# Attention and tree feed-forward on one core: which PSUM bank a tile gets is chosen by a count of each engine's work

## The chip, the cores and the metric

The kernel runs on one core of a Trainium2 chip. The metric is the device time of one execution in microseconds (us), smaller is better. TensorE is called PE, its weight loads PEld, VectorE DVE, ScalarE ACT, GpSimd POOL and SyncE, which issues the DMAs, SP.

## The reference

Eight sequences of 512 tokens and 256 features pass through four residual layers, each behind a layer norm:

```python
x = x + attn_a(layernorm(x), ...)   # 16 heads of 16, biases, every key is seen
x = x + ffn(layernorm(x), ...)
x = x + attn_b(layernorm(x), ...)   # 16 heads of 16, rotary embedding, causal
x = x + ffn(layernorm(x), ...)      # the same weights as above
```

`attn_a` and `attn_b` are softmax(q k / sqrt(16)) v with an output projection. `ffn` is a soft decision tree of depth 8: gate = sigmoid((x Wq) routers), 255 gates a token; the probability of each of 256 leaves is the product of the gates (or one minus the gate) on its path; the result is leaf_prob @ leaf_values, projected by Wout with a bias. All is in float32.

## The kernel before, in words

The work is cut into 16 blocks n: n = 0 to 7 are the sequences' first attention and tree, n = 8 to 15 the causal attention and the tree again. The main loop at the end of `hybrid_kernel` goes over steps i. Every step issues, in this order:

- `scores`: four PSUM tiles named st, one for each of four row groups of 32 partitions (four heads side by side), k times q in two passes and a third that subtracts the row maximum from rows in m. ACT then takes exp of each tile into pt (L599); in the causal blocks POOL masks pt (L604).
- `maxima`: four PSUM tiles named mx, q times k in two passes, one tile for each row group. DVE takes the largest of each row (L554 non-causal; L549 in the causal blocks, with the mask). This runs some seven steps ahead of the scores.
- `weigh`, once in four or fewer steps: the tile av, pt times v, copied by ACT (L621).
- other units of work, put between by tables of due steps written out by hand (BEFORE, BEHIND, OUTPUT, CHAINS): the projections v, q and k, the output projection y, the gates z, the tree's product ty and the transposes xt, txt and lt, each with a PSUM tile of its own.

`passes` issues the four tiles' first matmuls, then their second, and so on, so that the four row groups work at the same time:

```python
    for i in range(last + 1):
        for parts in todo:
            ps, lhsT, rhs = parts[part][i]
            nc.tensor.matmul(ps, lhsT=lhsT, rhs=rhs, start=i == 0, stop=i == last)
```

Its matmuls are L516 in the profile, of mx and st alike. Those of v, y, z and ty are L376 (`by_tokens`), of the transposes L350, of q and k L418 and L490, of av L616.

Who reads a PSUM tile: ACT reads st (L599), av (L621), the transposes (L351, L359), v (L458), z (L727, tanh) and the non-causal q and k (L426). DVE reads mx (L554, L549), adds y and ty to x (L669) and multiplies the causal q and k with cosine and sine (L498). DVE also multiplies the tree's paths (L756, lp<-th,lp), which reads no PSUM.

Every PSUM tile comes from `bank`. There is one pool of eight buffers under one tag, and each tile fills a whole bank:

```python
    banks = ctx.enter_context(tc.tile_pool(name="banks", bufs=8, space=PSUM))
    def bank(shape, name):
        return banks.tile(shape, F32, tag="ps", name=name)
```

The framework's pool chooses which of the eight buffers a tile gets when it builds the program, and puts semaphore waits on the tile's first matmul for the last reader of the buffer's former tile. After the whole program is written, `in_program_order` ties each engine's instructions to the order in which they were written, so no instruction overtakes another on its engine.

## Time and profile before

| | |
|---|---|
| median of 3 runs | 1142.22 us (1135.12 to 1142.41) |
| the profiled execution | 1138.38 us |
| its span | 1136.5 us |
| PE busy | 1047.8 us, 92% |
| DVE busy | 835.5 us, 74% |
| ACT busy | 630.2 us, 55% |
| POOL busy | 435.4 us, 38% |
| mean granted PE clock | 0.971 |

The span is the time from the first to the last instruction that the profiler recorded; the execution's own time has 1.9 us around it. All rows come from one profiled execution. In lists of groups, a row gives the line, engine, operation, output and input tiles with their shapes, the number of instructions, then busy time, mean ns of one instruction, and the idle time of the engine just before them with what ended most of it. In the timeline, a row gives the start, the duration of a run of like instructions, and in brackets the idle time before it and its releaser. PE matmuls overlap one another in the records, and their ends are modelled.

### The profile page before, as it was taken

Reading aid. Unit: us, or ns where it says so; the run is one execution under the profiler, and the core shown is the slowest. Engines: PE = TensorE matmul, PEld = TensorE weight load, DVE = VectorE, ACT = ScalarE, POOL = GpSimd, SP = SyncE. Lnnn points to the kernel's source line nnn. Section 1 sums busy time; section 2 is a strip of 40 time slices with the busy share of each in tenths; the row PEclk is TensorE's granted clock in tenths of the full one; section 3 lists DMA queues with packets and bytes.
Section 4 is the critical chain, followed back from the end, with each engine's and each line's share of the span. In section 5 each row is a group of like instructions: output and inputs, shape, how many; then the busy total and the mean of one; then the engine's idle time right before and its main releaser. Section 6 shows DMA issues by size and latency. Waiting matters only on the chain. (4 is left out here: it accounts for less than half of the span.)

```text
span 1136.5 us, 24276 instructions
## 1 busy us (share of the span) xinstructions
PE 1047.8 (92%) x8916; PEld 608.4 (54%) x8916; DVE 835.5 (74%) x2368; ACT 630.2 (55%) x1329; POOL 435.4 (38%) x600
## 2 busy tenths in 40 slices
PE   5999999999999999999999898999999999999886
PEld 2544454554545545455454555656555565556555
DVE  4867586767767777777867868887878787887735
ACT  2466666666666666666474544554455455545441
POOL 2221332222412224122325464655456465554242
PEclk9999999999999999999999999999999999999799
DMA  8110302104031040321222304131221404140111
GB/s 305 66 59 18 132 22 103 42 17 164 22 117 60 21 164 23 128 74 36 96 78 75 102 29 148 41 125 67 100 87 43 140 22 152 40 146 23 41 36 56
DMA packets 69671, 91.48 MB, mean 80 GB/s; under 512 B 15025, under 2 KB 36273, under 8 KB 69553
## 3 DMA queue, kind: packets, MB, share of 16 engines
q1 hardware_dynamic: 69552, 89.94, 22.9%
q8 instruction: 70, 1.15, 0.4%
q14 instruction: 49, 0.39, 0.1%
HBM read 20.71 MB, written 8.91 MB: 26 GB/s over the span
## 5 line engine op out<-in xcount | busy, mean ns | idle before, releaser
L599 ACT ACTIVATE pt<-st 128x512 f32<-128x512 f32 (+1 forms) x896 | 435.0, 573 | 205.3 <-PE st L516 203.7
L554 DVE TENSOR_REDUCE most<-mx 128x1 f32<-128x512 f32 x512 | 317.0, 682 | 120.1 <-PE mx L516 119.8
L549 DVE CUSTOM_DVE_ANT_0 seen<-mx,mask 128x128 f32<-128x128 f32 (+3 forms) x512 | 250.5, 489 | 85.6 <-PE mx L516 37.9
L516 PE MATMUL mx<-k,q 32*128 32x512 f32 (+3 forms) x2048 | 221.2, 395 | 35.4 <-DVE most L549 10.6
L616 PE MATMUL av<-pt,v 128*32 128x512 f32 (+3 forms) x2048 | 200.2, 531 | 6.4 <-DVE x L669 2.8
L516 PE MATMUL st<-q,k 32*128 32x512 f32 (+3 forms) x2048 | 187.4, 402 | 2.8 <-DVE most L549 1.8
L516 PEld LDWEIGHTS mx<-k,q 32*128 32x128 f32 x2048 | 128.4, 187 | 90.3 <-DVE most L549 23.0
L604 POOL TENSOR_SCALAR_AFFINE_SELECT pt<-pt 128x256 f32<-128x256 f32 (+1 forms) x192 | 97.7, 517 | 165.3 <-ACT pt L599 163.1
L388 POOL TENSOR_TENSOR hl<-r,hl 128x512 fp32r<-128x512 f32 x62 | 80.2, 1300 | 179.8 <-ACT hl L426 168.8
L516 PEld LDWEIGHTS st<-q,k 32*128 32x128 f32 x2048 | 90.7, 185 | 108.5 <-issue 69.4
L616 PEld LDWEIGHTS av<-pt,v 128*32 128x32 f32 x2048 | 62.7, 112 | 131.0 <-issue 94.5
L621 ACT COPY o<-av 128x512 f32<-128x512 f32 x64 | 37.5, 586 | 137.3 <-issue 106.5
L516 PE MATMUL st<-m,ones 32*128 32x512 f32 (+3 forms) x1024 | 101.2, 356 | 0.0
L756 DVE SCALAR_TENSOR_TENSOR lp<-th,lp 128x8 f32<-128x8 f32 (+7 forms) x238 | 74.5, 350 | 3.8
L502 POOL TENSOR_TENSOR r<-r,r 128x512 f32<-128x512 f32 x32 | 41.4, 1303 | 85.9 <-DVE r L498 85.9
L376 PE MATMUL ty<-wl,lpT 128*128 128x256 f32 x256 | 67.6, 416 | 2.4 <-ACT lpT L359 1.4
L376 PE MATMUL z<-wg,txnT 128*128 128x255 f32 x256 | 63.1, 390 | 3.4 <-ACT pt L599 2.5
L418 PE MATMUL qk<-xnT,a_qk 128*128 128x512 f32 x128 | 63.4, 624 | 0.9 <-ACT pt L599 0.7
L662 POOL TENSOR_TENSOR out<-out,den 128x512 f32<-128x512 f32 x31 | 40.4, 1304 | 61.2 <-DMA den<-apart 55.1
L490 PE MATMUL qk<-xnT,b_qk 128*128 128x512 f32 x128 | 59.4, 605 | 2.9 <-ACT xnT L351 2.5
L516 PEld LDWEIGHTS st<-m,ones 32*128 32x128 f32 x1024 | 57.5, 185 | 6.5 <-DMA m<-rows 0.7
L376 PEld LDWEIGHTS ty<-wl,lpT 128*128 128x128 f32 x256 | 51.4, 207 | 15.0 <-issue 2.8
(86 smaller groups left out, 1075.2 us busy)
## 6 DMA issues: line engine op xcount, KB each, us to landing
q<-hl SPq DMA_DIRECT2D x128, 256.0 KB
k<-hl SPq DMA_DIRECT2D x64, 256.0 KB
out<-o SPq DMA_DIRECT2D x64, 128.0 KB
den<-apart SPq DMA_DIRECT2D x32, 256.0 KB
x<-x SPq DMA_DIRECT2D x8, 512.0 KB
between<-x SPq DMA_DIRECT2D x8, 512.0 KB
x<-between SPq DMA_DIRECT2D x8, 512.0 KB
out<-x SPq DMA_DIRECT2D x7, 512.0 KB
```

The source lines that it names most:

```text
L376: nc.tensor.matmul(ps[:, i, :n], lhsT=srcT[:, c, (t + i) * P : (t + i + 1) * P], rhs=w[:, c, :], start=c == 0, stop=c == NC - 1,)
L388: on.tensor_tensor(hl[:, 1, :], raw, hl[:, 0, :].bitcast(F32), ALU.subtract)
L418: nc.tensor.matmul(ps, lhsT=(w.q, w.k)[which][:, k, c * P : (c + 1) * P], rhs=xnT[:, k, :], start=k == 0, stop=k == NC - 1,)
L490: nc.tensor.matmul(ps, lhsT=wt[:, k, c * P : (c + 1) * P], rhs=xnT[:, k, :], start=k == 0, stop=k == NC - 1,)
L502: nc.gpsimd.tensor_tensor(raws[c], raws[c], raws[2 + c], (ALU.subtract, ALU.add)[c])
L516: nc.tensor.matmul(ps, lhsT=lhsT, rhs=rhs, start=i == 0, stop=i == last)
L549: nc.vector.tensor_tensor_reduce(out=seen[:, :width], in0=ps, in1=mask[:, S - width :], scale=1.0, scalar=LOWEST, op0=ALU.add, op1=ALU.max ...
L554: nc.vector.tensor_reduce(at, ps, AX.X, ALU.max)
L599: nc.scalar.activation(pt[:, i, :at], ps[:, :at], AF.Exp, scale=SCALE)
L604: nc.gpsimd.affine_select(out=blocks, in_=blocks, pattern=[[0, 2], [0, len(kts)], [1, P]], compare_op=ALU.is_ge, fill=0.0, base=0, channel ...
L616: nc.tensor.matmul(av[32 * j : 32 * j + 32, first:], lhsT=vs[n % 2][:, kt, g * NJ + j, :, :].rearrange("p d s -> p (d s)"), rhs=pts[j // 2 ...
L756: nc.vector.scalar_tensor_tensor(pairs[:, :, :, side], of_level, one, lp[:, part, :], ALU.add, ALU.mult)
```

## The change

Instead of one pool with eight buffers there is one pool with a single buffer under each of eight tags, ps0 to ps7, and a class `Banks` that names the tag. While the program is written it keeps a running count of time for PE, ACT and DVE. `take` gives a tile the bank whose expected free time is the smallest, and moves PE's count to that time if it is behind. `work` adds a cost to an engine's count. `read` says who reads a tile and for how long: the reader's count becomes the later of itself and PE's count plus LATE, plus the cost, and the bank is expected free LATE after that. The costs are six constants in us. Everything happens when the program is built; the calls of `work` and `read` are spread over the functions that issue matmuls and readers. POOL has no count, and a few operations of ACT and DVE that read no PSUM are not counted.

```diff
+PASS, PRODUCT, COPY, REDUCE, CHANGE, LATE = 0.25, 0.89, 0.58, 0.69, 0.15, 0.1
+class Banks:
+    def __init__(self, pool):
+        self.pool = pool
+        self.free = [0.0] * 8
+        self.taken = {}
+        self.at = dict(pe=0.0, act=0.0, dve=0.0)
+
+    def take(self, shape, name):
+        k = min(range(8), key=lambda i: self.free[i])
+        self.at["pe"] = max(self.at["pe"], self.free[k])
+        self.free[k] = float("inf")
+        t = self.pool.tile(shape, F32, tag=f"ps{k}", name=name)
+        self.taken[id(t)] = (k, t)
+        return t
+
+    def work(self, engine, cost):
+        self.at[engine] += cost
+
+    def read(self, t, *costs):
+        k, _ = self.taken.pop(id(t))
+        for engine, cost in costs:
+            self.at[engine] = max(self.at[engine], self.at["pe"] + LATE) + cost
+        self.free[k] = max(self.at[e] for e, _ in costs) + LATE
...
-    banks = ctx.enter_context(tc.tile_pool(name="banks", bufs=8, space=PSUM))
+    banks = Banks(ctx.enter_context(tc.tile_pool(name="banks", bufs=1, space=PSUM)))
-    def bank(shape, name):
-        return banks.tile(shape, F32, tag="ps", name=name)
+    bank = banks.take
...
     # layer_norm, for each of four tiles
+            banks.work("dve", COPY)
...
     # transposed
+        banks.work("pe", PRODUCT)
+        banks.read(ps, ("act", COPY))
...
     # by_tokens, then v, z and the adds of y and ty to x
+            banks.work("pe", count * PRODUCT)
+                banks.read(ps, ("act", count * COPY / 2))
+            banks.read(ps, ("dve", count * REDUCE / 2))
...
     # causal q and k
+                banks.work("pe", 2 * PRODUCT)
+                banks.read(ps, ("dve", 2 * REDUCE))
...
     # passes, once for each pass over the four row groups
+                banks.work("pe", PASS * todo[0][part][i][2].free_size() / S)
...
     # maxima
+        banks.work("pe", CHANGE)
+        for whole, parts in zip(blocks, got):
+            banks.read(whole, ("dve", sum(REDUCE * (width + 80) / (S + 80) for _, width, _ in parts)))
...
     # scores
+                banks.read(ps, ("act", COPY * (at + 80) / (S + 80)))
...
     # weigh
+        banks.work("pe", CHANGE + sum(PRODUCT * (S - first) / S for _, _, first in group))
+        banks.read(av, ("act", COPY))
...
     # the tree's levels
+                banks.work("dve", 0.1 + len(ts) * m * 0.002)
```

More of the change, by code (lines that the diff above doesn't have):

```diff
@@ L276, in chains @@
                     )
+                banks.work("pe", PRODUCT)
+                banks.read(ps, ("dve" if to is wl else "act", COPY))
                 if to is wl:
@@ L291, in fold_bias @@
         nc.vector.tensor_tensor(out_b, ps, out_b, ALU.add)
+        banks.work("pe", PRODUCT)
+        banks.read(ps, ("dve", COPY))
         folded.append(True)
@@ L351, in transposed @@
         nc.scalar.copy(dst[:, c, :], ps.rearrange("p t q -> p (t q)"))
+        banks.work("pe", PRODUCT)
+        banks.read(ps, ("act", COPY))
     def transposed_half(dst, src, ts, name):
@@ L359, in transposed_half @@
         nc.scalar.copy(dst[:, :, ts[0] * P : ts[0] * P + 2 * P], ps.rearrange("p c t q -> p c (t q)"))
+        banks.work("pe", PRODUCT)
+        banks.read(ps, ("act", COPY))
     def by_tokens(srcT, w, n, name, evict, times, ts=range(NT)):
@@ L426, in block @@
             nc.scalar.activation(to, ps, AF.Identity, bias=w.qk_b[:, at : at + 1])
+        banks.work("pe", 2 * PRODUCT)
+        banks.read(ps, ("act", 2 * COPY))
         return raw, hl
@@ L498, in pre @@
                     nc.vector.tensor_tensor(raws[-1], ps, table, ALU.mult)
+                banks.work("pe", 2 * PRODUCT)
+                banks.read(ps, ("dve", 2 * REDUCE))
             if causal:
@@ L528, in maxima @@
         most = lesses[n, g]
-        got, todo = [], []
+        got, todo, blocks = [], [], []
+        banks.work("pe", CHANGE)
         for j in range(NJ):
@@ L532, in maxima @@
             rows = slice(32 * j, 32 * j + 32)
+            blocks.append(ps)
             got.append([])
@@ L569, in put @@
         nc.scalar.copy(rows, ps)
+        banks.work("pe", PASS)
+        banks.read(ps, ("act", COPY / 2))
         nc.sync.dma_start(ms[g % 2].bitcast(F32)[:: HD, :], rows)
@@ L647, in divide @@
         inv = pool2.tile([P, S // HD], F32, tag="inv", name=f"inv{n}_{c}")
+        banks.work("dve", COPY)
         nc.vector.reciprocal(inv, few[:, c, :])
@@ L729, in gates @@
             )
+            banks.read(ps, ("act", count * COPY / 2))
         yield from by_tokens(xnT, wg, NODES, f"z{n}", gates, when(n, "z"), ts)
```

## The prediction

> **What bounds the kernel now.** I read the page's busy shares first, then busy time by stretch, then the costliest groups, and then followed the PSUM banks tile by tile through the timeline: of each tile, when the last reader of the bank's former tile ended and when the tile's own first matmul began.

> ```profile
> span 1136.5 us, 24276 instructions
> PE 1047.8 (92%) x8916; PEld 608.4 (54%) x8916; DVE 835.5 (74%) x2368; ACT 630.2 (55%) x1329; POOL 435.4 (38%) x600
> ...
> L599 ACT ACTIVATE pt<-st 128x512 f32<-128x512 f32 (+1 forms) x896 | 435.0, 573 | 205.3 <-PE st L516 203.7
> L554 DVE TENSOR_REDUCE most<-mx 128x1 f32<-128x512 f32 x512 | 317.0, 682 | 120.1 <-PE mx L516 119.8
> ...
> L516 PE MATMUL mx<-k,q 32*128 32x512 f32 (+3 forms) x2048 | 221.2, 395 | 35.4 <-DVE most L549 10.6
> ```

> PE is busy 92% and idle 88.7 us. ACT and DVE mostly wait for PE, and PE in its turn waits ahead of mx matmuls: short waits for a reader to give a bank back. The idle column understates them, since a matmul whose four row groups do not start together still counts as busy. By the bank bookkeeping 576 of 2229 tiles start within 0.15 us of their bank's release, 0.05 to 0.06 us behind it, and the matmuls of these groups start some 130 us later in all than in groups whose banks were free.

> ```profile
> 40.00:570.00 530.00, 504.67 (x4092) 269.04 (x4096) 387.88 (x800) 341.66 (x688) 146.93 (x169) 1.00 0.21 73
> 570.00:1075.00 505.00, 466.70 (x4395) 291.56 (x4386) 395.65 (x1424) 259.72 (x585) 258.61 (x375) 0.96 0.24 82
> ```

> (Columns: stretch, its length, busy time of PE, PEld, DVE, ACT, POOL, granted clock, DMA share, GB/s.) The first row is the non-causal stage, the second the causal one. DVE's share is 73% and 78%: near enough to full that DVE's queue, not the choice of a bank, ends many PE waits.

> **The change part by part.** *Eight pools and the count.* They add no instruction: compiled, each engine has the same instructions in the same order as before, no DMA issue is moved past another, and all 2229 tiles come in the same order. Only the bank of a tile differs, and with it the reader that its first matmul waits for: 1054 tiles follow another tile than before in their bank. Price of the code itself: 0.

> *What a choice can be worth.* Four mx or st tiles form a group, whose second pass is issued behind the first pass of all four, so the latest of four banks sets the group. At the times of this trace the best possible choice would take 16.1 us off these waits. The new choice takes 11.4 us off 14 larger and 6 small groups, and makes 47 groups later by 20.9 us together. What remains is to say which of both survive.

> *Loss 1, the projection y.* In the stretch where y is interleaved with the last two mx groups of a sequence, the timeline shows:

> ```profile
> 487.77 0.93 PE L516 MATMUL mx<-k,q 32*128 32x512 f32 x8
> 488.51 2.48 DVE L554 TENSOR_REDUCE most<-mx 128x1 f32<-128x512 f32 x4 [0.60 <-PE mx L516]
> 488.63 1.99 PE L376 MATMUL y<-a_o,out 128*128 128x256 f32 x8
> 490.55 0.74 PE L516 MATMUL st<-q,k 32*128 32x512 f32 x8
> 490.91 0.68 DVE L669 TENSOR_TENSOR x<-y,x 128x512 f32<-128x512 f32 x1
> 491.35 1.02 PE L516 MATMUL mx<-k,q 32*128 32x512 f32 x8
> 491.55 2.06 ACT L599 ACTIVATE pt<-st 128x512 f32<-128x512 f32 x4 [1.52 <-PE st L516]
> 491.65 0.29 PEld L516 LDWEIGHTS mx<-k,q 32*128 32x128 f32 x5 [0.33 <-DVE x L669]
> 492.30 1.99 PE L376 MATMUL y<-a_o,out 128*128 128x256 f32 x8
> ```

> The fourth mx tile takes y's bank: the add ends at 490.91 + 0.68 = 491.59, the tile starts at 491.64. The changed kernel gives it the bank of the first st tile, whose exp ends at 491.55 + 0.60 = 492.15: it starts 0.55 late (492.20). In the next group (495.32) the same swap costs 0.61. Why the count errs, from the start of the earlier mx group: it puts y's release at 4.35 us (four reads of REDUCE 0.69, where the trace has 2.48/4 = 0.62; two LATE) and the exp's at 4.01 (its PE takes 2.47 to the st group); the trace has 3.82 (487.77 to 491.59) and 4.38. It is off by 0.53 one way and 0.37 the other, and turns a lead of 0.56 into a lag of 0.34. Behind the late tile stand pass two, then y (1.99, held by PE alone), then st, whose exps and reads start at fixed distances behind PE; nothing there has the slack to give the time back, and DVE and ACT, which wait 0.6 and 1.5 us here, are only later too. Sequences 1 to 6: 6 x (0.55 + 0.61) = 7.0; sequence 7: 0.25 + 0.61 = 0.9. Sum 7.9 us.

> *Loss 2, other non-causal groups.* Two with ty in y's place (0.69, 0.68) and two small ones (0.25, 0.18) stand ahead of PE work as well: 1.8, taken as 1.6. Those early in sequences 0 and 1 (0.36, 0.32, 0.57, 0.81) come ahead of a group that waits longer for its reader anyway: 0, and 2.1 if that cover is missing.

> *Loss 3, causal.* The third mx group's bank moves to v's copy or the last sequence's first exps (2.3 over six sequences, kept 1.9); single groups at 709.38 (0.51), 1031.49 (kept 0.55 of 0.90), 1072.88 (kept 0.4 of 0.69), 637.19 (kept 0.3 of 0.51): together 3.7, taken as 3.6. The rest (st groups of 0.2, lessT, 626.30, 632.30; 3.1) is ahead of a longer wait for DVE: 0 under that cover.

> *Gains.* The largest repeats in five causal sequences:

> ```profile
> 744.43 0.32 PE L516 MATMUL mx<-k,q 32*128 32x128 f32 x1 [0.32 <-DVE r L498]
> 745.63 0.72 PE L516 MATMUL mx<-k,q 32*128 32x128 f32 x13 [0.87 <-DVE r L498]
> 745.49 1.39 DVE L756 SCALAR_TENSOR_TENSOR lp<-th,lp 128x512 f32<-128x512 f32 x1
> 750.20 1.28 DVE L669 TENSOR_TENSOR x<-ty,x 128x512 f32<-128x512 f32 x2
> ```

> The fourth tile would start 0.97 earlier, 5 x 0.97 = 4.9 us. But DVE works without a gap from 743.10 to 751.48; its reads of these tiles stand behind lp and cannot come earlier. PE gains 0.97 and stands at the next mx group, whose third tile waits for the second ty add (ends 751.48, tile starts 751.53) whenever PE arrives. So 0, with 4.9 as the other bound. Kept are one group at 665.53, where DVE itself is idle 0.89 for PE (1.0), and about half of the 2.03 at 1054.40, where the next bank's reader then binds (1.0): 2.0. Six non-causal gains of 0.3 to 0.5 come, like the covered losses, ahead of a longer wait: 0, at most 2.3.

> *Sum.* 7.9 + 1.6 + 3.6 - 2.0 = +11.1 us. The profiled execution took 1138.38 us with a span of 1136.5 (1.9 around it, unchanged): 1149.5. Against the median of the runs shown, 1142.22, it would be 1153.3; of the four executions two lie at 1142.3, one at 1135.1 and this one at 1138.4. I say 1150.0, nearer the one whose steps I followed.

> [...] The row at 491.65 shows PE waiting for one bank's reader with seven others taken, and by it the choice counts.

> **The rivals.** *B, nothing is absorbed:* each late group costs PE what the trace says, since what follows it shifts as well: 1138.4 + 20.9 - 2.0 = 1157.3. For it: PE is at 92%. Against: DVE's 78% in the causal stage.

> *C, not slower:* the mis-picks of y are void, because in the changed run exp does end before y's add, as the count has it. From an order of 0.56 us the other way this decides: the add must come 0.56 later, or the exp earlier, than in the trace; the gains then stand whole, 1138.4 - 11.4 = 1127.0. For it: ACT has 45% idle. Against: exp and add hang on PE's starts with distances that repeat in seven sequences.

> *D, it does not do what it says:* DVE and ACT queues set the pace so far that any choice gives the same time; bank numbers are mostly labels: 1138.4 to 1142.2, within 2 us. For it: most changed tiles had a bank free long before in both kernels (only 72 tiles' new bank is still held at the trace's start of the tile). Against: the waits of 491.65 follow the reader at once.

> **How the numbers follow.** My forecast (+5 to +16 us, 1143 to 1158) 0.65, B 0.15, C 0.08, D 0.12. Predicted: 1150.0. The range goes from 1139 (losses half absorbed, or D) to 1160 (B with the runs' own spread). One per cent is 11.4 us, about what a measurement of this kernel can tell from no change. Faster: C, 0.08. Slower by over 1%: B and half of the forecast, 0.15 + 0.32 = 0.47. Within: 0.45.

> **What would show it.** In the changed profile, around the y motif, PEld or PE of mx should wait for ACT pt L599's new line instead of DVE x, about 0.85 us instead of 0.33, in sequences 1 to 7; PE waits for "DVE r" in the causal stage should fall by some 5 us while those for DVE's maxima and x adds grow by as much; DVE's and ACT's busy time should be unchanged, PE's idle time plus its stretched mx matmuls some 11 us higher, of them 9 before 570 us. I am wrong if y's add is not ahead of the exp there, if the non-causal stage is not longer, or if the causal stage is shorter by more than 2 us.

## The result, and the profile after

The changed kernel takes 1144.8 us (median of 20 runs) against 1138.57 us before (20 runs): ratio 1.0049, 95% interval 1.0028 to 1.0069, or +5.6 us (3.2 to 7.9). A second comparison (after_again, below) gave 1.0054. I had forecast +11.1 us: the sign held, and the size was twice what came.

The page of the changed kernel, profiled in an execution of 1147.6 us (its lines answer to those shown of before; line numbers moved):

```profile
span 1145.7 us, 24268 instructions
PE 1049.0 (92%) x8916; PEld 607.6 (53%) x8916; DVE 834.6 (73%) x2368; ACT 631.3 (55%) x1329; POOL 434.3 (38%) x600
...
L654 ACT ACTIVATE pt<-st 128x512 f32<-128x512 f32 (+1 forms) x896 | 435.0, 573 | 203.9 <-PE st L563 202.2
L606 DVE TENSOR_REDUCE most<-mx 128x1 f32<-128x512 f32 x512 | 317.3, 682 | 132.6 <-PE mx L563 131.9
...
L563 PE MATMUL mx<-k,q 32*128 32x512 f32 (+3 forms) x2048 | 230.7, 400 | 43.5 <-ACT pt L654 16.7
```

The work of every engine is what it was. The mx matmuls are 9.5 us longer in the records (221.2 to 230.7) and PE stands 8 us more ahead of them (35.4 to 43.5), the largest part now for ACT's exp. The list of PE's waits shows the exchange (engine, line, released by: us in total, times, longest):

```profile
PE mx L563 <- ACT pt L654: 16.7, 38, 1.2
PE mx L563 <- DVE most L601: 10.9, 28, 1.1
...
PE lessT L619 <- DVE less L611: 4.0, 6, 1.0
```

Of mx for ACT it was 2.7 us before, for DVE r (causal q and k) 10.4 and now 1.4, of av for DVE x 2.8 and now none among its longer waits. The wait of lessT for DVE is new.

The y motif of sequence 6, in the timeline of the changed kernel:

```profile
502.14 0.74 PE L563 MATMUL st<-q,k 32*128 32x512 f32 x8
...
502.50 0.68 DVE L727 TENSOR_TENSOR x<-y,x 128x512 f32<-128x512 f32 x1
...
502.94 0.41 PE L563 MATMUL mx<-k,q 32*128 32x512 f32 x3
503.13 2.06 ACT L654 ACTIVATE pt<-st 128x512 f32<-128x512 f32 x4 [1.63 <-PE st L563]
503.78 0.29 PEld L563 LDWEIGHTS mx<-k,q 32*128 32x128 f32 x5 [0.87 <-ACT pt L654]
...
504.43 1.99 PE L417 MATMUL y<-a_o,out 128*128 128x256 f32 x8
```

y's bank is free at 502.50 + 0.68 = 503.18, but the fourth mx tile has the first st tile's bank, free at 503.13 + 0.60 = 503.73, and starts at 503.78: 0.55 late, as reckoned. The y behind it starts 0.55 late too.

Both kernels issue the same matmuls in the same order, so the start of each tile can be subtracted between the two traces. The changed kernel's delay is 1.4 us at 100 us, grows by 0.55 and 0.61 at the y groups of each of sequences 2 to 6, is 14.5 us where the causal stage begins (585 us), and then shrinks to 9.2 us. Two jumps of 1.7 us in it lie where the changed trace has half clock (granted clock 0.72 on the mean from 137 to 143 us of its own time, 0.66 from 347 to 352). The causal stage, where I expected +1.6, came out 5.3 us shorter in this pair of traces. That was one of the signs by which I had said I would be wrong. Not all of it is banks: the trace before spends 51.2 us of that stage at half clock, the changed one 37.5.

Ratios of the further runs, each against before on the same chip, in us of 1138.5:

| run | ratio | 95% interval | us |
|---|---|---|---|
| old_choice | 0.9994 | 0.9974 to 1.0014 | -0.7 |
| only_y | 1.0053 | 1.0028 to 1.0078 | +6.0 |
| not_y | 0.9975 | 0.9947 to 1.0002 | -2.8 |
| by_trace | 0.9969 | 0.9949 to 0.9989 | -3.5 |
| causal_new | 0.9988 | 0.9969 to 1.0008 | -1.4 |
| gains | 0.9983 | 0.9963 to 1.0004 | -1.9 |
| losses | 1.0042 | 1.0026 to 1.0059 | +4.8 |
| calibrated | 0.9973 | 0.9949 to 0.9997 | -3.1 |
| y_late | 1.0299 | 1.0266 to 1.0331 | +34.0 |
| rest_nc | 1.0021 | 1.0000 to 1.0041 | +2.4 |
| after_again | 1.0054 | 1.0025 to 1.0083 | +6.1 |
| warm_old | 0.9940 | 0.9916 to 0.9963 | -6.8 |
| warm_new | 1.0005 | 0.9984 to 1.0025 | +0.6 |
| warm_trace | 0.9909 | 0.9879 to 0.9938 | -10.4 |

### The profile page after: what moved, and what is told of

Its sections match the earlier page's. It is cut to its first block, busy times and chain, and to the rows that moved or that the text cites. A ratio compares the mean times of both kernels' runs of the same rounds, so it can differ in the third digit from the quotient of the medians.

```text
span 1145.7 us, 24268 instructions
## 1 busy us (share of the span) xinstructions
PE 1049.0 (92%) x8916; PEld 607.6 (53%) x8916; DVE 834.6 (73%) x2368; ACT 631.3 (55%) x1329; POOL 434.3 (38%) x600
## 5 line engine op out<-in xcount | busy, mean ns | idle before, releaser
L654 ACT ACTIVATE pt<-st 128x512 f32<-128x512 f32 (+1 forms) x896 | 435.0, 573 | 203.9 <-PE st L563 202.2
L563 PE MATMUL mx<-k,q 32*128 32x512 f32 (+3 forms) x2048 | 230.7, 400 | 43.5 <-ACT pt L654 16.7
L563 PE MATMUL st<-q,k 32*128 32x512 f32 (+3 forms) x2048 | 183.1, 403 | 2.4 <-DVE most L601 1.5
L676 ACT COPY o<-av 128x512 f32<-128x512 f32 x64 | 37.5, 586 | 144.8 <-issue 107.6
L549 POOL TENSOR_TENSOR r<-r,r 128x512 f32<-128x512 f32 x32 | 41.3, 1303 | 87.0 <-DVE r L543 87.0
L417 PE MATMUL ty<-wl,lpT 128*128 128x256 f32 x256 | 64.3, 400 | 3.6 <-ACT lpT L398 1.4
L360 POOL TENSOR_SCALAR ln_lesst<-ln_mvt 128x4 f32<-128x4 f32 (+1 forms) x17 | 4.1, 239 | 148.8 <-DVE ln_mvt L353 148.8
```

The lines of the kernel that those rows point to most:

```text
L417: nc.tensor.matmul(ps[:, i, :n], lhsT=srcT[:, c, (t + i) * P : (t + i + 1) * P], rhs=w[:, c, :], start=c == 0, stop=c == NC - 1,)
L549: nc.gpsimd.tensor_tensor(raws[c], raws[c], raws[2 + c], (ALU.subtract, ALU.add)[c])
L654: nc.scalar.activation(pt[:, i, :at], ps[:, :at], AF.Exp, scale=SCALE)
```

## The experiments

Most of them replace the count by a list: one digit, the bank, for each of the 2229 tiles. The list is the choice of one kernel, with exchanges of two banks' digits from some tile on.

```diff
+TABLE = ("0123456...", ...)
     def take(self, shape, name):
-        k = min(range(8), key=lambda i: self.free[i])
+        k = int(TABLE[len(self.seen)])
+        self.seen.append(name)
```

### The parts of the change

**old_choice**: the list of the kernel before.

> The class with its eight pools, but the banks are read from a list: the choice of the kernel before, tile by tile. Both theories (a late bank costs PE its time in full; part of it is given back by fewer stretches at half the PE clock): no change, ratio 1.000 within 0.003, and the profile's waits as before. If the eight pools cost something by themselves: about 1.005, as the changed kernel.

-0.7 us (-3.0 to +1.6), no change: no cost of eight pools of one buffer can be told from nothing, and 0.5% is excluded. What the change does is in who gets which bank.

**only_y**: that list, with 14 exchanges.

```diff
-    mx6_3_2_3 follows y5_0 in its bank       (and 13 like it)
+    mx6_3_2_3 follows st6_1_3_0
```

> The old choice from the list, with 14 exchanges alone: the fourth mx tile of the last two mx groups of sequences 1 to 7 gets the first st tile's bank, as in the changed kernel, instead of y's. By the trace these cost 7.9 us. Theory 1 (every late bank costs in full, the y groups are the bulk of the loss): ratio 1.007 (+7.9 us), and in the profile +1.16 us for each sequence. Theory 2 (the delays are there, but the clock gives part back: fewer or cheaper stretches of half clock): +1.16 us for each sequence outside those stretches, but the ratio only 1.003 to 1.005. Rival (the loss is elsewhere, in the causal stage): 1.000 to 1.002.

+6.0 us (3.2 to 8.9). In its trace the delay grows again by 0.55 and 0.61 at the y groups of each of sequences 2 to 6.

**not_y**: the changed kernel's list with the same 14 put back.

> The changed kernel's choice from a list, with the 14 fourth mx tiles behind y put back to the bank of the kernel before. Theory 1: 7.9 us less than the changed kernel; against before 1.0049 - 0.0069 = 0.998. Theory 2: about half of that is seen, 1.001. Rival (the loss is elsewhere): 1.004 or more.

-2.8 us, 8.4 below the changed kernel's +5.6. With only_y it brackets the 7.9 of the forecast: loss 1 stood. And it leaves a surprise: without the y tiles the change is not 3.2 us slower, as the rest of my sum says, but level or a little faster (-6.0 to +0.2).

**rest_nc** and **causal_new** split this rest: not_y's list up to 585 us and the old one behind it; the old list up to 585 us and the changed kernel's behind it.

> The changed kernel's choice of the non-causal stage without the 14 tiles behind y, and the old choice from 585 us on: what I called loss 2 and the early gains. By the trace of before 4.7 us later and 3.3 earlier. My sum kept 1.6 us of it: ratio 1.0014. If, as not_y (0.9975) less causal_new (0.9988) hints, nothing is lost there: 0.998 to 1.000.

> Old choice up to 585 us (from the list), the changed kernel's choice behind it: the causal stage alone, its losses and gains together. My sum for this stage (losses kept 3.6, gains kept 2.0): +1.6 us, ratio 1.0014. If the stage gives back more than I counted, which not_y at 0.9975 hints at: -2 to -4 us, 0.997 to 0.998. If nothing of the gains stands and all losses do: +7 us, 1.006.

The non-causal rest costs 2.4 us (1.6 forecast), the causal stage -1.4 (+1.6 forecast). only_y, rest_nc and causal_new add up to +7.0; the whole was +5.6 and +6.1. So the choice of banks divides into parts that add up, within their intervals, and the one part that lies outside the forecast by more than its interval (-3.5 to +0.9) is the causal stage.

**losses** and **gains** divide that stage once more.

> Old choice, with only the changed kernel's later banks in the causal stage (third mx group, first mx groups at 709.4 and 1031.5 us, st groups, lessT; 7.8 us by the trace of before). My count: those ahead of a longer wait for DVE are absorbed, 3.6 us stay, 1.003. If nothing is absorbed: 1.007. If DVE's queue absorbs all: 1.000.

> Old choice, with only those ten exchanges of the changed kernel that make a causal bank come free earlier: five mx groups behind the causal q and k (4.9 us), three av tiles (3.0), the mx group at 665.5 us (1.1) and the st group at 1054.4 us (2.0). No tile waits longer than before by the trace of before. If a wait ahead of a busy DVE is only moved, as I reckoned for the first five and would for av: -2 to -3 us, 0.9974 to 0.9982. If the gains stand whole: -11 us, 0.990. If the av tiles are kept as well: -5 us, 0.9956.

losses: +4.8 of a possible 7.8, near the 3.6 reckoned. gains: -1.9 of a possible 11, as reckoned (2.0). The trace of gains shows the absorption where the prediction put it, at the group behind the causal q and k (before first, then gains):

```profile
743.09 0.51 PE L516 MATMUL st<-q,k 32*128 32x256 f32 x8
746.28 3.72 PE L376 MATMUL ty<-wl,lpT 128*128 128x256 f32 x16
751.53 0.30 PEld L516 LDWEIGHTS mx<-k,q 32*128 32x128 f32 x6 [0.40 <-DVE x L669]
```

```profile
739.63 0.51 PE L592 MATMUL st<-q,k 32*128 32x256 f32 x8
742.14 3.72 PE L446 MATMUL ty<-wl,lpT 128*128 128x256 f32 x16 [0.24 <-DVE r L572]
748.06 0.30 PEld L592 LDWEIGHTS mx<-k,q 32*128 32x128 f32 x6 [0.41 <-DVE x L756]
```

gains is 3.46 us ahead at st and 4.14 at ty, and 3.47 again at the next mx group, which waits for the second ty add: the lead is handed back there.

Each alone is what the absorption argument says, yet together (causal_new) they give -1.4 rather than +2.9. With some 2 us of interval on each of the three this is at the edge of what they can tell. The traces show one reason. At 650 us of before, av waited 1.0 us for y's add; the changed kernel takes this away and PE then stands at lessT, whose input comes from DVE. In the aligned traces the delay falls by 1.02 at that av and rises by 0.59 at the mx group behind it, which is one of my "kept" losses, and by 0.66 at lessT. By the bookkeeping the loss alone costs PE 0.6; with the gain ahead of it, it only fills the wait at lessT. I had reckoned the losses on a trace that lacked the new gaps.

**by_trace**: the bank that was free first by the trace of before. **calibrated**: the changed kernel with four constants read off that trace.

```diff
-PASS, PRODUCT, COPY, REDUCE, CHANGE, LATE = 0.25, 0.89, 0.58, 0.69, 0.15, 0.1
+PASS, PRODUCT, COPY, REDUCE, CHANGE, LATE = 0.25, 0.96, 0.515, 0.62, 0.15, 0.055
```

> Banks from a list: each tile gets the bank that was released first by the times of the profile of before. Static bookkeeping: 16.1 us of mx and st waits and three waits of av of 1.0 us less, nothing later. Theory 1 with absorption (a wait ahead of a busy DVE is only moved): 3 to 6 us are kept, ratio 0.995 to 0.997. Rival (the gains stand whole): 19 us, 0.983.

> The changed kernel with four constants from the profile of before: PRODUCT 0.96 (y's 1.92 us to the next group, two products), COPY 0.515 (2.06/4), REDUCE 0.62 (2.48/4), LATE 0.055 (start behind release). The count then puts y's bank first again; by the trace of before 3.9 us of waits are later and 12.9 us (with three av waits) earlier. If the y groups are the bulk of the loss and most gains are absorbed: 0.996 to 0.999, 6 to 9 us less than the changed kernel. If wrong constants were not the cause: 1.004.

-3.5 and -3.1 us. Even a choice made with the trace in hand keeps a fifth of the 19 us that its bookkeeping promised. The count's idea was sound and its prices were not: 0.07 us on each reduction and each product, adding up over a step, turned its order around at y. Four numbers read off the profile move it by 9 us (1.0049 to 0.9973). In the calibrated kernel's trace the fourth mx tile follows y's add again:

```profile
497.07 0.68 DVE L727 TENSOR_TENSOR x<-y,x 128x512 f32<-128x512 f32 x1
497.80 0.29 PEld L563 LDWEIGHTS mx<-k,q 32*128 32x128 f32 x5 [0.34 <-DVE x L727]
```

The wait is 0.34 us for the add, as before, where the changed kernel has 0.87 for the exp.

### What the parts leave open: the clock

**y_late** was meant to tell whether a late bank costs PE in full, by a larger dose.

```diff
-    mx6_3_2_3 follows st6_1_3_0              (only_y)
+    mx6_3_2_3 follows st6_1_3_2
```

> As only_y, but the 14 fourth mx tiles get the third st tile's bank, released 0.98 us behind the first's: 21.6 us by the trace of before, 3.1 us a sequence, nothing else changed. Theory 1 (a late bank here costs PE in full): +21.6 us, ratio 1.0190. Theory 2 (part is given back by fewer stretches of half clock, as only_y's 6.0 of 7.9 may hint): 14 to 17 us, 1.012 to 1.015, and fewer half-clock stretches than the 19 to 21 of the kernels with the old choice.

+34.0 us: neither theory allowed more than the 21.6 of the late banks. The timeline of sequence 2 shows what came on top:

```profile
216.73 0.40 PE L592 MATMUL mx<-k,q 32*128 32x512 f32 x3
218.55 0.73 PE L592 MATMUL mx<-k,q 32*128 32x512 f32 x5 [1.43 <-ACT pt L683]
219.21 2.84 PE L446 MATMUL y<-a_o,out 128*128 128x256 f32 x8
221.98 1.22 PE L592 MATMUL st<-q,k 32*128 32x512 f32 x8
```

After a wait of 1.43 us the same eight y matmuls take 2.84 us instead of 1.99, and st 1.22 instead of 0.74: the granted clock went to half (0.54 on the mean from 220.5 to 223.9 us, the figure behind the five engines).

```profile
220.50:223.90 3.40, 3.40 (x19) 1.83 (x17) 2.69 (x7) 0.19 (x1) 0.00 (x0) 0.54 0.00 0
```

The kernel before has such places too. Busy time by stretch around one of its long waits for the causal q and k, 805.5 us on (stretch, length, busy PE, PEld, DVE, ACT, POOL, granted clock, DMA share, GB/s):

```profile
805.50:808.90 3.40, 2.23 (x42) 1.81 (x42) 3.40 (x7) 1.81 (x5) 1.48 (x2) 1.00 0.01 2
808.90:812.30 3.40, 3.40 (x9) 2.71 (x9) 2.75 (x15) 1.06 (x2) 3.40 (x4) 0.50 0.01 2
```

PE is idle for 1.17 of 3.4 us, and has half its clock for the next 3.4. In the trace of before half clock comes in 15 stretches: eleven of 3.413 us, one of 6.827 and two of 10.240, and one that the trace's end cuts short; in that of the changed kernel in 13 (eight, two and two, and one cut short). Within each trace all of them start on one grid of 3.413 us. It lies differently against the program in the two: one half-clock stretch starts at 126.24 us of before, one at 128.76 us of the changed kernel. At full clock the starts of products of 128x512 elements in float32 lie 0.429 us apart in both traces, and those of two passes of the mx groups (q and k, float32r, 512 elements, four row groups together) 0.22 us at the least. With half the price for q and k as for float32, and the part of the array's rows and columns that a matmul uses, I added up the matmuls of each grid window as a share of 3.413 us. The windows at full clock that were followed by half clock (15 and 13) had a share of 0.39 or less in before and 0.35 or less in the changed kernel; of those followed by full clock 3 of 295 and 5 of 301 had 0.39 or less. So in these two traces half clock follows a grid window with little PE work. Whether a place with little work fills such a window goes with where the grid lies; what else may set the half clock off is not shown. From these shares I estimate some 11 to 12 entries (a window at full clock followed by half clock) between 40 and 1050 us for the trace of before, which has 10, and 8 to 9 for that of the changed kernel, which has 7. Some of the long waits that are gone in the causal stage had stood in such windows, as at 805.5 us. But single profiles of one choice scatter as widely as this difference, as the next two show.

**after_again** and **before_again** (this for its profile alone) are the second profile of the one and the third of that choice.

> The changed kernel once more, on the same chip as y_late and rest_nc. If the first comparison was right: 1.0049 within 0.003. By the sum of the parts measured since (only_y 1.0053, causal_new 0.9988, rest near 1): 1.004. By my forecast: 1.0097. Theory 2 expects fewer half-clock stretches in its profile than with the old choice (19 and 21), as in the first one (18).

> The kernel before once more, for its profile: the number and place of half-clock stretches. Theory 2: 19 or more; otherwise they scatter between 16 and 25 whatever the choice of banks.

+6.1 us, between what the parts add up to and the first result. The stretches of half clock in the whole span come to 61.4 and 51.2 us in the changed kernel's two profiles, 64.8, 71.7 and 75.1 us in the three of the old choice: fewer, with a wide scatter.

The granted clock of every execution is on record as well, and says more than single traces. Twice the missing share of the clock, times the span, is the time at half clock. It is 63.9 us on the mean of 104 executions of the kernel before (48 to 78) and 56.4 us in 32 of the changed kernel (41 to 76): 7.5 us less, some 4 either way. Within one kernel, executions with more half clock are longer, by 0.34 us for each us of it (one slope fitted through all kernels without the unread products of the next runs). So about 2.6 us of the changed kernel's shortfall is the clock, and at equal half clock it is +8.4 us. Compared in the same way, only_y is +5.9, not_y +0.5, rest_nc +1.5, causal_new -0.9, losses +3.6, gains -1.7, by_trace -4.6, calibrated -3.5 and y_late +24.7. These are estimates from a fit, with 1 to 2 us of interval each. Why the changed kernel has less half clock stays open: causal_new (62.5 us) and gains (63.2) have no less than before.

**warm_old**, **warm_new** and **warm_trace** test it by filling waits. They issue products that nobody reads, no longer than the PE wait of the group in the trace.

```diff
+    def warm(name, ps):
+        for _ in range(WARM.get(name, 0)):
+            nc.tensor.matmul(ps[:, :D], lhsT=ident, rhs=wl[:, 0, :], start=True, stop=True)
...
+        warm(f"mx{n}_{g}_{qts[0]}", blocks[0])
         passes(todo)
```

> Old choice, and ahead of 30 mx and st groups (mx1_2_3, mx4_2_3, then the groups with long bank waits from 575 us on) 64 extra products of ident and wl into the group's first bank, which the group then overwrites: 0.43 us each, no more than the PE wait there holds. Bank waits end when they did. Clock theory: about 8 of the 11 half-clock entries between 40 and 1050 us go, worth 1.0 to 1.5 us each: 8 to 12 us less, ratio 0.990 to 0.993. Rival (the half-clock stretches come by chance or cost nothing): 1.000, or above where a product is in the way.

> The changed kernel with 55 such products ahead of 29 groups, by its own waits. Clock theory: it has fewer half-clock entries to lose (about 8 expected, of which some 5 are covered): 5 to 7 us less than the changed kernel, 0.999 to 1.001 against before, and 8 to 11 us above warm_old, which is the forecast of the banks alone. Rival: 1.005, and 5 to 6 us above warm_old.

> The choice by the trace (0.9969 before) with 51 such products ahead of 26 groups. Clock theory: 5 to 8 us less than without, 0.990 to 0.993, at best level with or below warm_old. Rival: 0.997.

warm_old does 64 products more than before and is 6.8 us faster, less than the 8 to 12 expected. Its timeline and clock at the wait for the causal q and k, as above:

```profile
744.13 1.56 PE L621 MATMUL mx<-wl,ident 128*128 128x256 f32 x6
745.62 0.90 PE L630 MATMUL mx<-k,q 32*128 32x128 f32 x16
```

```profile
805.00:808.40 3.40, 3.40 (x39) 2.13 (x40) 3.26 (x9) 1.64 (x4) 0.68 (x1) 1.00 0.03 7
808.40:811.80 3.40, 3.40 (x29) 2.95 (x27) 2.90 (x12) 0.62 (x1) 3.40 (x4) 1.00 0.01 2
```

Before, three of the group's sixteen matmuls had started by 744.43 and thirteen stood until 745.63; here all sixteen start from 745.62 on, in a trace that lies 0.20 us later at the st ahead (743.29 for 743.09), and ty follows at 746.45 for 746.28. The bank is no earlier; PE is only not idle until then, and in the stretch that had half its clock before it keeps the whole. In its executions half clock comes to 27.5 us for 65.7 of the kernel before in the same comparison. At 0.34 us each that would be 13 us (an estimate, and outside the range the slope was fitted in), so some 6 us may be lost again where products are in the way; no run shows where. The profiled executions granted 0.989 (warm_old) and 0.991 (warm_new) on the mean, for 0.971 of before. warm_new is 5.5 us below the changed kernel's second run. warm_trace, -10.4 us, has the lowest median of all, with the choice by the trace and filled waits; its interval overlaps that of warm_old.

With the clock mostly out of the way, warm_new stands 0.0065 above warm_old, +7.4 us (about 4 to 11 by the two intervals), where the plain kernels differ by 5.6. That is on the way to the 11.1 of the banks alone, and not shown to be there; the two also fill different groups, with 55 and 64 products.

## Why the prediction was wrong

*The reading of what bounds the kernel* stood: PE's waits for single banks moved as the bookkeeping said, tile by tile, and no other engine's work changed.

*Loss 1* stood: 0.55 and 0.61 us at the tiles named, nothing given back behind them; 6.0 us and 8.4 us by two experiments for 7.9. The reason named stood as well, since four corrected constants undo it.

*Loss 2* stood within the interval: 2.4 (0 to 4.7) for 1.6.

*Loss 3 and Gains* are the first step that failed: together -1.4 (-3.5 to +0.9) for +1.6, which is 3.0 of the 5.5 us by which I was high. Alone the two came out as reckoned (+4.8 for 3.6, -1.9 for 2.0). What failed is the addition: each was sized on the old trace, and a loss that falls into a gap which a gain has opened costs nothing, as at lessT. I also left out three waits of av for y's add, 1.0 us each, that the list of PE's waits shows (2.8 us, three times) and that the change removes. And the 1.0 that I kept of the gain at 1054.40 was not kept: in the trace of gains the lead over before grows from 3.8 to 5.9 us there and is 3.8 again at the mx group 1.4 us later. How the 3.0 divides among these is not shown.

*The clock* is the second: the sum has no term for it, so it took the granted clock as unchanged. The changed kernel's executions have 7.5 us less half clock, which by the fit above is 2.6 us, and at equal half clock it is +8.4 for the forecast of +11.1. That filling waits raises the clock and shortens the time is shown by the warm runs (0.989, 0.991 and 0.987 in the profiled executions for 0.971 of before; 6.8, 5.5 and 6.9 us less than the same choices unfilled); the 2.6 is an estimate. It doesn't explain the causal stage's part: causal_new has as much half clock as before, and is -0.9 at equal half clock.

*Rivals.* B, nothing absorbed (+19), is excluded by both comparisons. C had y's add behind the exp; the timeline shows it 0.55 ahead. D, any choice does the same, is excluded by only_y against old_choice.

*The signs to look for.* mx waits for exp at y: 0.87 us as forecast. Waits for DVE r fell by 9 us rather than 5, and those for DVE's maxima (10.6 to 10.9) did not grow in the list. That does not speak against the absorption, which the trace of gains shows at 751.53 us: there the wait lies inside a group whose first tiles have started, and counts as busy. The non-causal stage is longer, as forecast; the causal one is shorter by more than 2 us in the traces, of which some 4.7 of 5.3 us would be the clock by the same fit (13.7 us less half clock).

All eight banks were in use in every run here, and the medians went from 1130 to 1173 us with the choice of banks and the filling of waits alone.

PE's idle time of 1.17 us in all within 3.4 (before, 805.5 us, a share of 0.28) and of 1.43 us (y_late, 217 us) was followed by half clock (0.50, and 0.54 on the mean of 3.4 us). No run sets the idle time and the light load around it apart.

## What to carry to other kernels

Where a plan chooses by expected times, read its constants off the profile as spacings from one start to the next (2.48 us for four reads), not as durations of one instruction: what decides is the order of two releases half a microsecond apart. Size a set of edits on a trace that already has the other edits in it, since losses and gains ahead of the same wait do not add. And if PE must wait a microsecond or more at low load, look at the granted clock of the next 3.4 us before pricing the wait; where the bank can take it, an idle product that ends before the wait does may be worth more than the better bank (warm_old took 6.8 us off, by_trace 3.5).
